# Six layers of local attention: the value and output weights of a head as one matrix

## The chip, the cores and the metric

The kernel runs on one core of a Trainium2 chip. The metric is the device time of one execution in microseconds (us); the kernel before has a median of 3638.47 us over 3 runs (3638.31 to 3640.38). Engine names are those of the profile: PE (matmul) and PEld (its weight loads), DVE (vector), ACT (scalar), POOL (GpSimd) and SP, which issues the transfers (DMA).

## The reference

The input is 8 sequences of 512 tokens with 128 features, all in float32. A first attention with polynomial weights and a normalisation comes first; the change leaves its computation alone. Then six layers follow, each of a local attention and a gated feed-forward part. The attention of a layer is what changes:

```python
DIM = 128; DEPTH = 6; HEADS = 16; DIM_HEAD = 64; WINDOW = 32; INNER = HEADS * DIM_HEAD

def local_attention(q, k, v):          # windows of 32 queries, each sees its own and the
    ...                                # previous window: 64 keys
    sim = jnp.einsum('bhwie,bhwje->bhwij', bq, bk2) * QK_SCALE
    sim = jnp.where(mask, -jnp.finfo(sim.dtype).max, sim)
    attn = jax.nn.softmax(sim, -1)
    out = jnp.einsum('bhwij,bhwje->bhwie', attn, bv2)
    return out.reshape(b, h, n, d)

def attn_layer(x, Wqkv, qs, ksc, Wo):
    qkv = x @ Wqkv
    q, k, v = jnp.split(qkv, 3, -1)
    ...
    q = l2norm(q) * qs
    k = l2norm(k) * ksc
    ...                                # rotary turn of q and k
    out = local_attention(q, k, v)
    out = out.transpose(0, 2, 1, 3).reshape(b, n, INNER)
    return out @ Wo
```

In the loop over layers, attention and feed-forward part each add their result to x after half of the features of x have been shifted by one token (the kernel keeps x shifted in `state`).

For one head the output is softmax(S) (X Wv) Wo, and by the rules of matrix products this equals (softmax(S) X) (Wv Wo). Wv of a head is 128 x 64 and Wo 64 x 128, so Wv Wo is 128 x 128.

## The kernel before

`state[b]` holds a sequence with its 128 features on partitions and 512 tokens along the row. The work of the six layers is cut into 192 units: 6 layers, 8 sequences, 4 blocks of 128 tokens (`j`). A loop over slots `t` (L766) runs a software pipeline: in slot `t` each step works on the unit `t - lag`, as written `at(t, lag, step)`. The order of PE's instructions is exactly that of the program (`manual_schedule`, L757); the other engines are ordered by the framework's scheduler, with a few orders forced by `issue_behind` (L87). A slot holds, in PE's order:

- `proj` (lag 0, L439): q and k of a unit, two matmuls of 512 columns each, into PSUM tiles of the tag "mm". DVE multiplies them by two rotary tables (L459, L467), ACT squares them (L475), POOL adds the two products (L482). Later DVE sums the squares (`sum_squares`), ACT and POOL form the lengths and POOL scales (`unit_length`, L498).
- `by_keys` (lag 2, L594): 8 transposes of the softmax weights `pe`, in two PSUM tiles of the tag "tr", each copied by ACT to `pT`.
- `out_project` (lag 3, L637): 8 matmuls with `wo` into `py`, a PSUM tile of the tag "s"; DVE adds the two halves to `state` (L647).
- `by_features` (lag 1, L532): 16 transposes of q and k, in four "tr" tiles, each copied by ACT (L548). Between them lie `weigh_values` (lag 2, L604), 64 small matmuls of 64 rows and 32 columns, into `po` of the tag "s", which DVE divides by the softmax sums (L621), and `values` (lag 0, L502), the projection of v into an "mm" tile.
- `spread` (lag 0, L512): ACT copies v; eight DMAs (seven where a block is the first of its sequence) lay out the 64 keys of each window in `v2`.
- for the last block of a sequence, one part of the feed-forward step in each of four slots: `feed_norm`, `feed_first`, `feed_middle` (12 matmul instructions of 512 columns), `feed_last`.
- `scores` (lag 1, L563): 64 small matmuls that add to a mask which ACT has put into `sp` (`masked`, L553, tag "s"). DVE takes the maxima (L580), ACT makes 16 exps with the maxima as bias (L584), DVE sums (L590) and inverts (L591).
- `out_by_features` (lag 2, L627): 8 transposes of the divided result `on`, copied by ACT to `oT` (L635).

PSUM is handed out by tags: "mm" has two buffers of two banks, "tr" two buffers of one bank, "s" one of two banks. A new tile of a tag takes the buffer of the one before last ("mm", "tr") or the last ("s"), and its first matmul waits until that one's readers are done. Every float32 matmul of the program is two matmul instructions on PE, each with its weight load; a transpose is one.

Two calls of `addr_align` in the slot loop (L780, L782) and two in `feed_hidden` move the address of PE's next instruction to a multiple.

Of the kernel before, what the change touches and what calls it, by code (L numbers as in the profile page):

```python
# [28 lines left out]
def sandwich_kernel(ctx: ExitStack, tc: tile.TileContext, ins: dict, out: bass.AP):  # L29
# [5 lines left out]
    DEPTH = ins["L0_ffn_Wqkv"].shape[0]  # L35
# [16 lines left out]
    x1 = [dram.tile([P, NB, DM], F32, tag=f"x1_{b}", name=f"x1_{b}") for b in range(B)]  # L52
    roots = [dram.tile([2, 2, 2, N], F32, tag=f"roots_{i}", name=f"roots_{i}") for i in range(2)]
    state = [const.tile([P, N + 1], F32, tag=f"state_{b}", name=f"state_{b}") for b in range(B)]
    for b in range(B):
        nc.vector.memset(state[b][HD:P, 0:1], 0.0)

# [95 lines left out]
    tw = wl.tile([P, 3, 2, 512], F32, tag="wqkv", name="tw")  # L153
# [4 lines left out]
    nc.sync.dma_start(tw[:, 2], a_w[:, 2])  # L158
# [3 lines left out]
    woT = tw[:, 2].rearrange("p s (c d) -> p (s c) d", d=DM)  # L162
# [200 lines left out]
    def to_state(b):  # L363
        xs = bt[b].pop("xs")
        ps = psum.tile([P, NB, P], F32, tag="tr", name="tr")
        for j in range(NB):
            transposed(ps[:, j, :], xs[:, j, :], P, P)
        pf = ps.rearrange("p a b -> p (a b)")
        for a in range(2):
            r = slice(HD * a, HD * (a + 1))  # L370
            nc.vector.tensor_copy(state[b][r, a : N + a], pf[r])

# [36 lines left out]
    def load_layer(l):  # L409
        wqkv = wl.tile([P, 3, 2, 512], F32, tag="wqkv", name=f"wqkv_{l}")  # L410
        nc.sync.dma_start(
            wqkv, ins["L0_ffn_Wqkv"][l].rearrange("p (t s c) -> p t s c", t=3, s=2)
        )
        wo = wl.tile([P, NP, DM], F32, tag="wo", name=f"wo_{l}")
        nc.sync.dma_start(wo, ins["L0_ffn_Wo"][l].rearrange("(c p) d -> p c d", p=P))
# [21 lines left out]
        return dict(wqkv=wqkv, wo=wo, w1=w1, w2=w2, tab=tab)  # L437

    def proj(u, s):  # L439

        L, b, j = u["L"], u["b"], u["j"]
        wqkv, tab = L["wqkv"], L["tab"]
# [7 lines left out]
        for a in range(2):  # L450
            nc.tensor.matmul(  # L451
                ps[:, a].rearrange("p h d -> p (h d)"), lhs, wqkv[:, s, a, :], start=True, stop=True
            )
# [30 lines left out]
    def sum_squares(u, s):  # L484
        su = nc.vector.tensor_reduce(  # L485
            u["ss"][:, s], u["sq", s].rearrange("p h a d -> p h (a d)"), AX.X, ALU.add
        )
        if divisions:
            issue_behind(su, divisions[-1])
# [12 lines left out]
    def values(u):  # L502
        L, b, j = u["L"], u["b"], u["j"]
        lhs = state[b][:, j * P : (j + 1) * P]

        v0 = f3.tile([P, 2, 512], F32, tag="v0", name="v0")
        ps = psum.tile([P, 2, 512], F32, tag="mm", name="mm")
        for p in range(2):
            nc.tensor.matmul(ps[:, p, :], lhs, L["wqkv"][:, 2, p, :], start=True, stop=True)  # L509
        u["v0"], u["v0ps"] = v0, ps  # L510

    def spread(u):  # L512
        j, v0 = u["j"], u["v0"]
        cp = nc.scalar.copy(v0, u.pop("v0ps"))
        if copies:
            issue_behind(cp, copies[-1])

        v2 = f2.tile([P, 4, 512], F32, tag="v2", name="v2")
        for p in range(2):
            if j == 0:  # L520
                nc.gpsimd.memset(v2[HD * p : HD * p + W, 0, :], 0.0)
            else:
                nc.sync.dma_start(v2[HD * p : HD * p + W, 0, :], u["B"]["v0"][P - W : P, p, :])
            nc.sync.dma_start(v2[HD * p + W : HD * (p + 1), 0, :], v0[0:W, p, :])
            for w in range(1, 4):
                nc.sync.dma_start(
                    v2[HD * p : HD * (p + 1), w, :], v0[W * (w - 1) : W * (w + 1), p, :]
                )
        u["B"]["v0"] = v0
        u["v2"] = v2  # L530
# [32 lines left out]
    def scores(u):  # L563
# [18 lines left out]
        for pair in range(NP):  # L582
            for p in range(2):
                ex = nc.scalar.activation(  # L584
                    pe[:, pair, p, :], sp[:, p, pair, :], AF.Exp, bias=mx[:, p, pair : pair + 1]
                )
                issue_behind(ex, tables[-1])
# [4 lines left out]
        u["pe"], u["su"] = pe, su  # L592
# [11 lines left out]
    def weigh_values(u):  # L604


        v2, pT, su = u["v2"], u["pT"], u["su"]
        po = psum.tile([P, 2, NP, HD], F32, tag="s", name="po", bufs=1)
        for pair in range(NP):
            for w in range(4):  # L610
                for p in range(2):
                    r = slice(HD * p, HD * (p + 1))
                    nc.tensor.matmul(  # L613
                        po[W * w : W * (w + 1), p, pair, :],
                        pT[r, pair, W * w : W * (w + 1)],
                        v2[r, w, HD * pair : HD * (pair + 1)],
                        start=(pair == 0), stop=True, skip_group_check=True,
                    )
        u["on"] = on = f1.tile([P, NP, 2, HD], F32, tag="on", name="on")
        with tc.high_priority():  # L620
            dv = nc.vector.tensor_tensor(  # L621
                on.rearrange("t c p d -> t p c d"), po,
                su.rearrange("t c p -> t p c").unsqueeze(3).to_broadcast([P, 2, NP, HD]), ALU.mult,
            )
        divisions.append(dv)

    def out_by_features(u):  # L627
        on = u["on"]
        u["oT"] = oT = f1.tile([P, NP, P], F32, tag="oT", name="oT")
        for c in range(0, NP, 4):  # L630
            ps = psum.tile([P, 4, P], F32, tag="tr", name="tr")
            for i in range(4):
                transposed(ps[:, i, :], on[:, c + i].rearrange("p a d -> p (a d)"), P, P)
            with tc.high_priority():
                nc.scalar.copy(oT[:, c : c + 4, :], ps)  # L635

    def out_project(u):  # L637

        L, b, j, oT = u["L"], u["b"], u["j"], u["oT"]
        py = psum.tile([P, P], F32, tag="s", name="py", bufs=1)  # L640
        for c in range(NP):
            nc.tensor.matmul(py, L["wo"][:, c, :], oT[:, c, :], start=(c == 0), stop=(c == NP - 1))  # L642
# [114 lines left out]
    with tc.manual_schedule(engines={mybir.EngineType.PE}):  # L757
# [8 lines left out]
        for t in range(len(units) + 7):  # L766
            if t < len(units):
                u = units[t]
                if u["l"] not in layers:
                    layers[u["l"]] = load_layer(u["l"])  # L770
                u["L"] = layers[u["l"]]


            gelus = 0 <= t - 5 < len(units) and units[t - 5]["j"] == NB - 1
            at(t, 0, proj, 0)
            at(t, 0, proj, 1)


            if t % NB == 1 and NB < t < len(units):
                nc.tensor.addr_align(128, offset=IN_STEP)  # L780
            if t % NB == 3 and NB < t < len(units):
                nc.tensor.addr_align(FILL)  # L782
            at(t, 2, by_keys)
            if gelus:
                gelu_only()
            at(t, 3, out_project)
# [3 lines left out]
            if t == 1:  # L790
                attn_out(B - 1)
            at(t, 1, by_features, 0)
            at(t, 2, weigh_values)
# [135 lines left out]
```

## Time and profile before

| | |
|---|---|
| median of 3 runs | 3638.47 us (3638.31 to 3640.38) |
| profiled execution, span | 3641.2 us |
| first attention | 0 to about 479 us |
| six layers, begin (479 to 583 us) | PE busy 84.99 of 104.00 us |
| six layers, steady (583 to 3560 us) | PE busy 2969.12 of 2977.00 us; DVE 2416.28, ACT 2419.42, POOL 1754.86 |
| last 81.2 us | PE busy 59.49 us |
| clock granted to PE, mean | 0.993 |
| transfers | 250.73 MB, mean 69 GB/s |

The rows of a profile give the start and the length of a group of equal instructions, the engine, the line of the program, what is written and read with its shape (partitions x elements; for PE the rows and columns of the array), and the count. In brackets stands the time for which the engine stood idle before the group, and what released it. The rows of the layers' costliest groups on the other engines:

```profile
L482 POOL TENSOR_TENSOR qk<-t,t 128x1024 f32<-128x1024 f32 x384 | 910.9, 2372 | 619.1 <-DVE t L467 424.7
L498 POOL TENSOR_TENSOR qk<-qk,ss 128x1024 f32<-128x1024 f32 x384 | 722.4, 1902 | 16.0
L584 ACT ACTIVATE pe<-sp,mx 128x64 f32<-128x64 f32 x3072 | 652.0, 381 | 2.4 <-DVE mx L580 2.3
L635 ACT COPY oT<-tr 128x512 f32<-128x512 f32 x384 | 205.5, 587 | 168.1 <-PE tr L70 165.5
```

Each gives the busy time in all, the mean of one in ns, and the idle time before. Other rows used later: L514 (v copy, 128x1024) 1019 ns; L558 (mask, 128x1024) 1028; L548 (copies of q and k, 128x512) 589; L475 (squares, 128x512) 605; L316 (square of 128x1024) 1057; L621 (division, 128x1024) 1225; L459 and L467 1219; L647 (64x128) 284.

### The profile page before, as it was taken

What the parts mean: (1) busy time and instruction counts of PE and PEld (TensorE: products, weight loads), DVE (VectorE), ACT (ScalarE), POOL (GpSimd) and SP (SyncE); (2) the same over time, 40 slices, a digit from 0 to 9 for tenths busy, and PEclk for the clock granted to TensorE, in tenths of its full rate; (3) what the DMA queues carried; (4) which work ended last, traced back from release to release, by engine and by line L of the source; (5) the groups of instructions that cost most, each with busy time, mean ns of one, the idle gap of its engine ahead of it and who ended that gap; (6) DMA issues with size and microseconds to landing.
All of it is one profiled execution on the core that took longest, in us unless ns stands there. A gap on an engine that the chain in (4) does not pass through costs nothing.

```text
span 3641.2 us, 153034 instructions
## 1 busy us (share of the span) xinstructions
PE 3575.2 (98%) x65184; PEld 2404.3 (66%) x65184; DVE 2796.4 (77%) x3915; ACT 2765.6 (76%) x6864; POOL 1843.6 (51%) x1311
## 2 busy tenths in 40 slices
PE   8999989999999999999999999999999999999997
PEld 4555556666766666676766766667676676766765
DVE  4555567887878788787887878878787887878885
ACT  4555557787888888888787888888878787887875
POOL 0000045555655556555565655556555565556652
PEclk9999999999999999999999999999999999999998
DMA  3121132222232222232222322223222222222221
GB/s 109 46 53 47 42 89 68 65 65 69 79 77 72 65 64 71 77 81 68 61 69 68 87 72 69 65 65 86 71 71 69 60 70 64 66 68 73 74 74 47
DMA packets 158598, 250.73 MB, mean 69 GB/s; under 512 B 33774, under 2 KB 54508, under 8 KB 157164
## 3 DMA queue, kind: packets, MB, share of 16 engines
q1 hardware_dynamic: 157932, 240.93, 25.2%
q8 instruction: 530, 8.68, 1.0%
q14 instruction: 136, 1.11, 0.1%
HBM read 41.31 MB, written 4.46 MB: 13 GB/s over the span
## 4 chain that ended last, share of the span: by engine, by line
PE 87%; ACT 9%; DVE 2%; issue 1%; DMA 1%; POOL 0%; SPq 0%; POOLq 0%; DVEq 0%; ACTq 0%
PE tr L70 19%; PE mm L451 14%; PE py L642 10%; PE mm L509 9%; PE po L613 8%; PE sp L572 6%; ACT pe L584 4%; PE mm L667 4%; PE mm L669 4%; PE y L299 3%; PE py L702 3%; PE sc L269 2%; PE po L348 2%; ACT L76 1%; PE vv L247 1%; ACT oT L635 1%
## 5 line engine op out<-in xcount | busy, mean ns | idle before, releaser
L482 POOL TENSOR_TENSOR qk<-t,t 128x1024 f32<-128x1024 f32 x384 | 910.9, 2372 | 619.1 <-DVE t L467 424.7
L498 POOL TENSOR_TENSOR qk<-qk,ss 128x1024 f32<-128x1024 f32 x384 | 722.4, 1902 | 16.0
L451 PE MATMUL mm<-wqkv,state 128*128 128x512 f32 x1536 | 700.3, 596 | 0.6 <-issue 0.6
L584 ACT ACTIVATE pe<-sp,mx 128x64 f32<-128x64 f32 x3072 | 652.0, 381 | 2.4 <-DVE mx L580 2.3
L459 DVE TENSOR_TENSOR t<-mm,tab 128x1024 f32<-128x1024 f32 x384 | 468.3, 1219 | 220.3 <-PE mm L451 214.9
L475 ACT ACTIVATE sq<-mm 128x512 f32<-128x512 f32 x768 | 420.6, 605 | 127.4 <-DVE t L467 120.9
L467 DVE TENSOR_TENSOR t<-mm,tab 128x1024 f32<-128x1024 f32 x384 | 468.1, 1219 | 5.9
L451 PEld LDWEIGHTS mm<-wqkv,state 128*128 128x128 f32 x1536 | 273.1, 190 | 289.8 <-issue 242.4
L485 DVE TENSOR_REDUCE ss<-sq 128x16 f32<-128x1024 f32 x384 | 448.4, 1209 | 0.1
L70 PE MATMUL tr<-ident,qk 128*128 128x128 f32 x3072 | 440.9, 276 | 1.8 <-ACT qT L548 0.8
L70 PEld LDWEIGHTS tr<-ident,qk 128*128 128x128 f32 x3072 | 351.3, 141 | 120.7 <-issue 56.3
L642 PE MATMUL py<-oT,wo 128*128 128x128 f32 x3072 | 379.3, 277 | 0.3 <-ACT oT L635 0.3
L642 PEld LDWEIGHTS py<-oT,wo 128*128 128x128 f32 x3072 | 368.1, 196 | 0.5 <-ACT oT L635 0.5
L509 PE MATMUL mm<-wqkv,state 128*128 128x512 f32 x768 | 362.9, 595 | 2.6 <-DVE t L467 2.6
L635 ACT COPY oT<-tr 128x512 f32<-128x512 f32 x384 | 205.5, 587 | 168.1 <-PE tr L70 165.5
L572 PEld LDWEIGHTS sp<-kT,qT 64*32 64x32 f32 x24576 | 264.2, 105 | 91.3 <-issue 54.3
L613 PE MATMUL po<-v,pT 64*32 64x64 f32 x24576 | 297.0, 225 | 9.6 <-issue 3.9
L548 ACT COPY qT<-tr 128x512 f32<-128x512 f32 x384 | 226.3, 589 | 99.6 <-PE tr L70 99.1
L613 PEld LDWEIGHTS po<-v,pT 64*32 64x32 f32 x24576 | 268.8, 105 | 46.0 <-PE tr L70 24.6
L572 PE MATMUL sp<-kT,qT 64*32 64x64 f32 x24576 | 297.6, 225 | 0.3 <-issue 0.3
L495 POOL TENSOR_SCALAR ss<-ss 128x32 f32<-128x32 f32 x192 | 54.7, 285 | 478.7 <-ACT ss L98 470.8
L548 ACT COPY kT<-tr 128x512 f32<-128x512 f32 x384 | 225.6, 588 | 74.8 <-PE tr L70 74.5
(110 smaller groups left out, 5243.9 us busy)
## 6 DMA issues: line engine op xcount, KB each, us to landing
v<-v SPq DMA_DIRECT2D x1152, 128.0 KB
v<-v SPq DMA_DIRECT2D x672, 64.0 KB
rs<-roots SPq DMA_DIRECT2D x64, 256.0 KB
wqkv<-in_L_ffn_Wqkv_dram SPq DMA_DIRECT2D x6, 1536.0 KB
wo<-in_L_ffn_Wo_dram SPq DMA_DIRECT2D x6, 512.0 KB
xin<-_attn_hidden_states_dram SPq DMA_DIRECT2D x8, 256.0 KB
xr<-_attn_hidden_states_dram SPq DMA_DIRECT2D x8, 256.0 KB
x<-xr SPq DMA_DIRECT2D x8, 256.0 KB
```

Source lines behind the costliest of these rows:

```text
L70: nc.tensor.transpose(ps[:cols, :rows], src, ident[:rows, :rows])
L451: nc.tensor.matmul(ps[:, a].rearrange("p h d -> p (h d)"), lhs, wqkv[:, s, a, :], start=True, stop=True)
L459: nc.vector.tensor_tensor(t2, ps[:, ::-1], tab[:, 2 * s + 1, j, :].rearrange("p (a d) -> p a d", a=2).unsqueeze(2) .to_broadcast([P, 2, H, ...
L467: nc.vector.tensor_tensor(t1, ps, tab[:, 2 * s, j, :].rearrange("p (a d) -> p a d", a=2).unsqueeze(2) .to_broadcast([P, 2, H, HF]), ALU.mult,)
L482: nc.gpsimd.tensor_tensor(qk[:, s].rearrange("p h a d -> p a h d"), t1, t2, ALU.add)
L498: nc.gpsimd.tensor_tensor(t, t, ss[:, i, :].unsqueeze(2).to_broadcast([P, H, HD]), ALU.mult)
L509: nc.tensor.matmul(ps[:, p, :], lhs, L["wqkv"][:, 2, p, :], start=True, stop=True)
L548: copies.append(nc.scalar.copy(dst, ps))
L572: nc.tensor.matmul(sp[W * w : W * (w + 1), p, pair, :], qT[HD * p : HD * (p + 1), pair, W * w : W * (w + 1)], kT[HD * p : HD * (p + 1), pa ...
L584: ex = nc.scalar.activation(pe[:, pair, p, :], sp[:, p, pair, :], AF.Exp, bias=mx[:, p, pair : pair + 1])
L613: nc.tensor.matmul(po[W * w : W * (w + 1), p, pair, :], pT[r, pair, W * w : W * (w + 1)], v2[r, w, HD * pair : HD * (pair + 1)], start=(pa ...
L642: nc.tensor.matmul(py, L["wo"][:, c, :], oT[:, c, :], start=(c == 0), stop=(c == NP - 1))
```

## The change

The value projection and its layout are dropped. Each layer multiplies the value and output weights of every head once (`value_weights` loads them, `value_products` makes 16 matrices of 128 x 128, `wm`). The softmax weights are divided by their sums before they are transposed (POOL), and then weigh the tokens themselves: `windows` reads, for every window, its 64 tokens from a copy of the sequence in DRAM (`xtok`), `weigh_tokens` multiplies, and `out_project` sends the 16 results through the 16 matrices. `to_tokens` writes the copy in DRAM after each layer. The 16 exps become a subtraction on DVE and one exp. `py` moves from the tag "s" to the tag "tr". The softmax steps get one slot more of lag, the two `addr_align` of the slot loop go, and the weights of a layer are loaded in the middle of the layer before.

```diff
+    xtok = [dram.tile([W + N + 1, DM], F32, tag=f"xtok_{b}", name=f"xtok_{b}") for b in range(B)]
...
     def load_layer(l):
-        wqkv = wl.tile([P, 3, 2, 512], F32, tag="wqkv", name=f"wqkv_{l}")
...
-        wo = wl.tile([P, NP, DM], F32, tag="wo", name=f"wo_{l}")
...
+        wqk = wl.tile([P, 2, 2, 512], F32, tag="wqk", name=f"wqk_{l}")
...
+    def value_weights(l):
+
+        wv = f1.tile([P, NP, DM], F32, tag="on", name="wv")
+        wo = f1.tile([P, NP, DM], F32, tag="oT", name="wo")
+        for s, t in enumerate((wv, wo)):
+            nc.sync.dma_start(t.rearrange("p c d -> p (c d)"), ins["L0_ffn_Wvo"][l, s])
+        wm = wl.tile([P, 2, NP, DM], F32, tag="wm", name=f"wm_{l}")
...
+    def value_products(l):
+        L = layers[l]
+        for c in range(0, NP, 4):
+            ps = psum.tile([P, 2, 4, DM], F32, tag="mm", name="wm")
+            for i in range(4):
+                for p in range(2):
+                    r = slice(HD * p, HD * (p + 1))
+                    nc.tensor.matmul(
+                        ps[:, p, i, :], L["wv"][r, c + i, :], L["wo"][r, c + i, :], start=True, stop=True,
+                        skip_group_check=True,
+                    )
+            nc.scalar.copy(L["wm"][:, :, c : c + 4, :], ps)
...
     def sum_squares(u, s):
...
-        if divisions:
-            issue_behind(su, divisions[-1])
...
-    def values(u):
...
-    def spread(u):
-        j, v0 = u["j"], u["v0"]
-        cp = nc.scalar.copy(v0, u.pop("v0ps"))
-        if copies:
-            issue_behind(cp, copies[-1])
...
+    def windows(u):
+
+        b, j = u["b"], u["j"]
+        t = f3.tile([P, 2, 512], F32, tag="v0", name="xw")
+        u["xw"] = xw = t[:, 0].rearrange("p (w d) -> p w d", d=DM)
+        x0 = xtok[b][j * P : j * P + W + P, :]
         for p in range(2):
...
+            nc.sync.dma_start(
+                xw[HD * p : HD * (p + 1)],
+                bass.AP(tensor=x0.tensor, offset=x0.offset, ap=[[DM, HD], [W * DM, 4], [1, DM]]),
+            )
+
+    def to_tokens(u):
+
+        b = u["b"]
+        ps = psum.tile([P, NB, P], F32, tag="tr", name="tr")
+        for j in range(NB):
+            transposed(ps[:, j, :], state[b][:, j * P : (j + 1) * P], P, P)
+        xt = f2.tile([P, N], F32, tag="ge", name="xt")
+        nc.scalar.copy(xt, ps.rearrange("p a b -> p (a b)"))
+        nc.sync.dma_start(
+            xtok[b][W : W + N, :].rearrange("(n p) d -> p n d", p=P), xt.rearrange("p (n d) -> p n d", d=DM)
+        )
...
-        for pair in range(NP):
-            for p in range(2):
-                ex = nc.scalar.activation(
-                    pe[:, pair, p, :], sp[:, p, pair, :], AF.Exp, bias=mx[:, p, pair : pair + 1]
-                )
-                issue_behind(ex, tables[-1])
+        with tc.high_priority():
+            nc.vector.tensor_tensor(
+                pe.rearrange("t c p k -> t p c k"), sp,
+                mx.unsqueeze(3).to_broadcast([P, 2, NP, 2 * W]), ALU.add,
+            )
+        pf = pe.rearrange("t c p k -> t (c p k)")
+        ex = nc.scalar.activation(pf, pf, AF.Exp)
+        issue_behind(ex, tables[-1])
...
+        divisions.append(
+            nc.gpsimd.tensor_tensor(pe, pe, su.unsqueeze(3).to_broadcast([P, NP, 2, 2 * W]), ALU.mult)
+        )
...
-    def weigh_values(u):
...
-    def out_by_features(u):
...
+    def weigh_tokens(u, half):
+
+        xw, pT = u["xw"], u["pT"]
+        if half == 0:
+            u["zT"] = f2.tile([P, 2, NP, P], F32, tag="v2", name="zT")
+        zT = u["zT"]
+        ps = psum.tile([P, 2, NP, 2 * W], F32, tag="mm", name="z")
+        for i in range(2):
+            w = 2 * half + i
+            for p in range(2):
+                r = slice(HD * p, HD * (p + 1))
+                nc.tensor.matmul(
+                    ps[:, p, :, W * i : W * (i + 1)], xw[r, w, :], pT[r, :, W * w : W * (w + 1)],
+                    start=(i == 0), stop=True, skip_group_check=True,
+                )
+        nc.scalar.copy(
+            zT[:, :, :, HD * half : HD * (half + 1)].rearrange("f p c t -> f (p c) t"),
+            ps.rearrange("f p c t -> f (p c) t"),
+        )
 
     def out_project(u):
 
-        L, b, j, oT = u["L"], u["b"], u["j"], u["oT"]
-        py = psum.tile([P, P], F32, tag="s", name="py", bufs=1)
-        for c in range(NP):
-            nc.tensor.matmul(py, L["wo"][:, c, :], oT[:, c, :], start=(c == 0), stop=(c == NP - 1))
+        L, b, j, zT = u["L"], u["b"], u["j"], u["zT"]
+        py = psum.tile([P, P], F32, tag="tr", name="py")
+        for p in range(2):
+            for c in range(NP):
+                nc.tensor.matmul(
+                    py, L["wm"][:, p, c, :], zT[:, p, c, :],
+                    start=(p + c == 0), stop=(p + c == NP),
+                )
...
-        for t in range(len(units) + 7):
+        for t in range(len(units) + 8):
...
+                if t % (NB * B) == NB * B // 2 and u["l"] + 1 < DEPTH:
+                    layers[u["l"] + 1] = load_layer(u["l"] + 1)
+                    value_weights(u["l"] + 1)
...
-            if t % NB == 1 and NB < t < len(units):
-                nc.tensor.addr_align(128, offset=IN_STEP)
-            if t % NB == 3 and NB < t < len(units):
-                nc.tensor.addr_align(FILL)
-            at(t, 2, by_keys)
+            at(t, 3, by_keys)
...
-            at(t, 3, out_project)
+            at(t, 4, out_project)
...
             at(t, 1, by_features, 0)
-            at(t, 2, weigh_values)
+            at(t, 3, weigh_tokens, 0)
             at(t, 1, by_features, 4, 0)
             at(t, 1, masked)
-            at(t, 0, values)
+            at(t, 3, weigh_tokens, 1)
...
             at(t, 1, by_features, 4, 1)
-            at(t, 0, spread)
...
+            at(t, 2, windows)
...
+            if t % (NB * B) == NB * B - 3 and t < len(units) and u["l"] + 1 < DEPTH:
+                value_products(u["l"] + 1)
...
+            if t < 8 + NB * B * (DEPTH - 1):
+                at(t, 8, to_tokens, ends=True)
             at(t, 1, scores)
...
-            at(t, 2, out_by_features)
```

The other steps of the feed-forward part and of the output follow with one slot more of lag. `to_state` also writes the first copy of the tokens to DRAM; the first layer's products are made in slot 2.

## The prediction

> **What bounds the kernel now.** I read the page's busy times and chain first, then TensorE's timeline of the layer stage, then two places where it stands still. In the page the reader is to see that PE is taken 98% of the span and that the chain stays on PE for 87% of it; of ACT's 9% the next view shows why it is not idle PE.
>
> ```profile
> PE 3575.2 (98%) x65184; PEld 2404.3 (66%) x65184; DVE 2796.4 (77%) x3915; ACT 2765.6 (76%) x6864; POOL 1843.6 (51%) x1311
> PE 87%; ACT 9%; DVE 2%; issue 1%; DMA 1%; POOL 0%; SPq 0%; POOLq 0%; DVEq 0%; ACTq 0%
> ```
>
> TensorE's timeline of one slot (one unit of each lag; the six feed-forward matmul groups are left out). Matmul spans overlap at their ends, so a group's cost is its start to the next group's start.
>
> ```profile
> 2028.17 3.60 PE L451 MATMUL mm<-wqkv,state 128*128 128x512 f32 x8
> 2031.61 1.06 PE L70 MATMUL tr<-ident,pe 128*128 128x128 f32 x8
> 2032.51 1.95 PE L642 MATMUL py<-oT,wo 128*128 128x128 f32 x16
> 2034.30 1.04 PE L70 MATMUL tr<-ident,qk 128*128 128x128 f32 x8
> 2035.38 1.58 PE L613 MATMUL po<-v,pT 64*32 64x64 f32 x128
> 2036.89 0.66 PE L70 MATMUL tr<-ident,qk 128*128 128x128 f32 x4
> 2037.38 1.88 PE L509 MATMUL mm<-wqkv,state 128*128 128x512 f32 x4
> 2039.10 0.60 PE L70 MATMUL tr<-ident,qk 128*128 128x128 f32 x4
> ...
> 2045.08 1.58 PE L572 MATMUL sp<-kT,qT 64*32 64x64 f32 x128
> 2046.59 1.09 PE L70 MATMUL tr<-ident,on 128*128 128x128 f32 x8
> 2047.52 3.60 PE L451 MATMUL mm<-wqkv,state 128*128 128x512 f32 x8
> ```
>
> Differences of starts: 3.44 + .90 + 1.79 + 1.08 + 1.51 + .49 + 1.72 + .44 + 1.51 + .93 = 13.81 us a slot, without a gap. Other engines are hidden; only PE's sum and new gaps in it count. There are 192 units (6 layers, 8 batches, 4 blocks).
>
> **PE work.** Removed per unit: the value projection (L509, 1.72), the weighing of values (L613, 1.51) and the transposes of `on` (.93): 4.16. Added: out_project goes from 8 to 16 products, one more 1.79. weigh_tokens has 8 products with 64 rows, 128 columns and 256 moving columns, each two instructions as every f32 product here. A pass of 512 columns costs .43 (3.44/8), of 256 so .215. The trace has no 64x128 tiles; the nearest rows are the attention stage's row tiles (32x128) and column tiles (128x64):
>
> ```profile
> 411.45 1.51 PE L299 MATMUL y<-am,tv 128*64 128x384 f32 x8
> 412.90 0.93 PE L269 MATMUL sc<-tq,tk 32*128 32x384 f32 x8
> 413.75 1.98 PE L238 MATMUL qk<-xlT,tw 128*128 128x512 f32 x4
> ```
>
> Eight passes of 384 columns would be 2.58 one by one. They took .85 in four row tiles (two sets at .32 plus .21) and 1.45 in two column tiles (four at .32 plus .17). So tiles run side by side and a burst costs about .2 more: a half of weigh_tokens is 4 x .215 + .2 = 1.05 and both 2.1. Ends: .86 a half if the extra vanishes, 1.9 if the two tiles take turns. I take 1.05, because both neighbours overlap fully. Work alone: -4.16 + 1.79 + 2.1, and .11 less where `po` no longer stands between transposes: about -.38 a unit, -73 us over 192.
>
> [...]
>
> **New gaps in PE.** Moving `py` from its own buffer ("s") into the two "tr" buffers is what I price highest. The order in a slot becomes: transposes of the first four pairs of pe (buffer 1), of the second four (buffer 2), py (buffer 1 again), four transposes of q (2), four of k (1, now held by py). Before, py lay elsewhere, and 1.79 of py or 1.5 of po always stood between the two uses of a buffer. How long a buffer needs after its last matmul shows where PE had nothing else to do:
>
> ```profile
> 506.13 0.60 PE L70 MATMUL tr<-ident,qk 128*128 128x128 f32 x4
> 507.49 0.63 PE L70 MATMUL tr<-ident,qk 128*128 128x128 f32 x4 [0.77 <-ACT qT L548]
> 508.80 0.66 PE L70 MATMUL tr<-ident,qk 128*128 128x128 f32 x4 [0.68 <-ACT kT L548]
> ```
> ```profile
> 3613.03 0.49 PE L70 MATMUL nx<-ident,state 128*128 128x128 f32 x3
> 3613.24 0.59 DVE L647 TENSOR_TENSOR state<-py,state 64x128 f32<-64x128 f32 x2 [1.70 <-PE py L642]
> 3613.88 0.33 PE L70 MATMUL nx<-ident,state 128*128 128x128 f32 x1 [0.36 <-DVE state L647]
> ```
>
> Four transposes plus ACT's copy (589 ns) turn a buffer round in 1.31; .44 is PE's own, so it is free .87 after its last transpose. py now comes .44 after it: a gap of .43. In the second view py ends at about 3612.93 (the weight loads of the next group start there), DVE adds both halves, and PE goes on at 3613.88: .95. Only the four q transposes (.44) cover it: a gap of .51. Together .94 a unit, 180 us. Ends: the first 0 to 1.0 (ACT may be in a 605 ns square), the second .2 to 1.7 (DVE may be in a 1219 ns product). I take the bare turn-rounds, since ACT and DVE have idle time in the slot. Queued behind DVE's wait for py are proj's products of the second half and the sums of squares, and behind those POOL's L482; PE asks for that PSUM buffer again at the second half of weigh_tokens, 3 us later.
>
> **ACT, DVE, POOL.** ACT loses 16 exps (16 x 381 overlapped, 3.39 by the timeline, 652 us in all), the v copy (1019) and two oT copies (587 each); it gains one exp of 128x1024 (nearest row: Square of that shape, 1057) and two z copies (1019 each): about -2.5 a unit. DVE swaps the division (1225) for the subtraction of the maximum (same shape, 1225). POOL gains one 128x1024 product (L498's 1902; L482's 2372 as the other end) on a 51% engine, and loses small memsets. None of these times is on PE's path by itself: 11 to 13 us a slot each against 14. Their latency (maximum, subtraction, exp, sum, reciprocal, POOL product: 1.2 + 1.2 + 1.1 + 1.2 + .25 + 1.9 = 6.9) is covered by by_keys moving one slot later; without that slot it would exceed proj's 3.44 by 3.5 a unit. It removes PE's present wait for the exps in the slots after gelus (at 2050.96 eight transposes take 1.17 rather than .90): 48 x .27 = -12 us.
>
> But ACT's work bunches at the slot's end. Between z0 and the scores' second half it copies z0 (1.02), q (.59), fills the mask (1.03) and copies k (.58), with z1's copy (1.02) free to come before k's; the line that put the v copy behind k's copy is gone. Where a slot has the long feed-forward matmuls before the scores this is covered; in one of four only .5 us of transposes lie there, and in the gelu slot a PSUM buffer waits for z1's copy. I take 1.0 for four slots, 48 us; ends 0 and 154 (.8 in every slot).
>
> **Transfers and small steps.** Per unit eight SBUF copies of v (some 1 MB) become two reads of DRAM (256 KB), one slot before use; SP, which now waits 911 us on PE for L523, becomes lighter. Cover: a whole slot of 14 us. If a transfer took longer, PE would wait for xw. The write of tokens to DRAM lies 23 slots before its first reader. Weight loads move to the middle of the layer before: nothing, as PE waits for no weights now either. to_tokens: 40 x .44 = 18 us. value_products: 16 products of 64x128 by 128 a layer, 2.2 (16 pairs at .112 and two bursts' .2), 6 x 2.2 = 13; one by one 22. One slot more of fill and drain: 10 (0 to 20; the drain's chain is longer by the POOL product and the longer py).
>
> **Instruction supply.** The slots' two alignments go. How PE starves without them shows in the first slots, which never had any:
>
> ```profile
> 521.47 1.22 PE L613 MATMUL po<-v,pT 64*32 64x64 f32 x102
> 524.59 0.43 PE L613 MATMUL po<-v,pT 64*32 64x64 f32 x26 [1.90 <-issue]
> ```
>
> Between 513 and 583 us such gaps and one stretched L509 add to .64 + 1.90 + 1.45 + .31 + 1.97 = 6.3 in five slots, 1.25 a slot. The fetches are 530 of 8.68 MB, 16 KB or 256 instructions of 64 bytes. From the burst's start to its resumption pass 3.1 us, so I reckon a block used up faster than that runs dry. Only blocks that begin within some 46 of the new slot's 416 instructions are that quick (the scores' 256 alone in 1.5 us): 46/256 of a start a slot, .8 short on average, .14 a slot, 27 us. Ends: 0 and the old rate, 240. [...]
>
> **Sum.** -73 + 180 - 12 + 48 + 18 + 13 + 10 + 27 = +211. On the profiled span of 3641.2 that is 3852; the median of the runs, 3638.47, lies 2.7 lower: **3850 us**.
>
> **Rivals.** *A, no gaps, faster:* ACT and DVE release the "tr" buffers within the .44 that covers them. Then gaps and bunching (228) go, and with no starving (27) the sum is -44: 3595. It decides only if both releases come under .44; the 1.31 turn-round and the .95 speak against it. Chance .07. *B, row tiles of 64 take turns:* weigh_tokens costs 1.9 a half, +1.7 a unit, +326: 4175. Speaks for it: no such tile in the trace; against: both neighbours. Chance .08. *C, starving at the old rate:* +213: 4060. For: no alignment is left in the slot; against: one dense burst rather than two. Chance .07. *D, only one of the two gaps or neither bunching:* about 3640 to 3720, the PE saving nearly paid back. Chance .08, of it .03 within .2% of before. The forecast, gaps in every slot: .70, with its own range 3720 to 4020.
>
> The chances: faster by over .2% (7 us, about what these runs can tell from no change) .08, within it .03, slower .89. The range 3720 to 4020 leaves .2 outside.
>
> **What would show it.** Right: gaps of about .4 ahead of py released by ACT's pT copy, and of .5 ahead of k's transposes released by DVE's state; py groups of 3.58; z groups near 1.05; ACT well under 76%; PE's busy share below 95%. Wrong: PE without gaps (A), z groups near 1.9 (B), long `issue` gaps inside the scores (C). A scheduling of ACT or DVE that answers py a whole operation late would put the time above 4000.

## The result and the profile after

The kernel after takes **4052.3 us** (median of 4 runs, 4047.59 to 4053.91), the kernel before beside it 3638.73 us (4 runs, 3638.31 to 3640.38). The ratio is 1.1132, 95% interval 1.1117 to 1.1148: slower by 413.6 us where 211 were forecast. The profiled execution has a span of 4052.1 us at a mean granted clock of 0.987 (before: 3641.2 at 0.993).

The page of the kernel after, busy times and the chain that ended last:

```profile
PE 3712.4 (92%) x44800; PEld 2488.4 (61%) x44800; DVE 2785.3 (69%) x3916; ACT 2356.4 (58%) x3844; POOL 2140.6 (53%) x1407
PE 70%; ACT 15%; DVE 9%; issue 4%; DMA 1%; POOL 1%; SPq 0%; POOLq 0%; DVEq 0%; ACTq 0%
```

PE lost a third of its instructions and 6 points of its busy share, and the chain now leaves PE for ACT and DVE in a quarter of the span. PE's idle time went from 66.0 us (3641.2 - 3575.2) to 339.7 (4052.1 - 3712.4). That is 274 of the 411 us between the two spans; the other 137 stand as more busy time, although the work per unit fell. Part of it is the new steps `to_tokens` and `value_products`, and part is how the rows are made: a group's span reaches some .1 to .2 us into what follows it (in the view below .16 at `proj`, 3.70 long and 3.54 from start to start), so that a gap shows as idle time only past that tail. A gap is read from start to start, not from the bracket.

PE's timeline of one slot of the kernel after (start, length, line, operation, count; in brackets the idle time and its releaser), the one in which `feed_norm` (`nx`) and `to_tokens` run, then the scores and the next slot's `proj`:

```profile
2207.72 3.70 PE L479 MATMUL mm<-wqk,state 128*128 128x512 f32 x8
2211.26 1.04 PE L75 MATMUL tr<-ident,pe 128*128 128x128 f32 x8
2212.53 3.84 PE L655 MATMUL py<-zT,wm 128*128 128x128 f32 x32 [0.24 <-ACT pT L627]
2216.21 0.60 PE L75 MATMUL tr<-ident,qk 128*128 128x128 f32 x4
2217.15 0.63 PE L75 MATMUL tr<-ident,qk 128*128 128x128 f32 x4 [0.34 <-DVE state L663]
2217.70 1.13 PE L640 MATMUL z<-pT,xw 64*128 64x256 f32 x8
2218.77 0.66 PE L75 MATMUL tr<-ident,qk 128*128 128x128 f32 x4
...
2220.91 0.60 PE L75 MATMUL nx<-ident,state 128*128 128x128 f32 x4
2221.35 0.60 PE L75 MATMUL tr<-ident,state 128*128 128x128 f32 x4
2222.06 0.86 PE L592 MATMUL sp<-kT,qT 64*32 64x64 f32 x64
2223.49 0.86 PE L592 MATMUL sp<-kT,qT 64*32 64x64 f32 x64 [0.57 <-ACT kT L568]
2224.28 1.98 PE L479 MATMUL mm<-wqk,state 128*128 128x512 f32 x4
2228.14 1.98 PE L479 MATMUL mm<-wqk,state 128*128 128x512 f32 x4 [1.88 <-DVE xn L117]
```

Four things are to be seen. The two forecast gaps are there: 1.27 from `tr<-pe` to `py` instead of .90, and .94 from the q transposes to the k transposes instead of .44. A half of `weigh_tokens` costs 1.07. The scores wait between their halves for ACT's copy of k. And the second half of the next slot's `proj` comes 3.86 us after the first instead of some 1.7: it waits for `xn`, a product of the feed-forward norm on DVE, which the forecast didn't mention. DVE's timeline in that stretch shows why `xn` is late:

```profile
2224.46 1.23 DVE L600 TENSOR_REDUCE mx<-sp 128x16 f32<-128x1024 f32 x1 [1.74 <-PE sp L592]
2225.60 0.40 DVE L117 TENSOR_SCALAR xn<-nx,ln_mv,ln_rs 128x128 f32<-128x128 f32 x1
2225.92 1.22 DVE L603 TENSOR_TENSOR pe<-sp,mx 128x1024 f32<-128x1024 f32 x1
2227.05 1.04 DVE L117 TENSOR_SCALAR xn<-nx,ln_mv,ln_rs 128x128 f32<-128x128 f32 x3
```

After the maxima DVE makes one of the four `xn`, then the new subtraction (1.22), then the other three. `nx` and `proj`'s second half share the two "mm" buffers, so PE waits until the last `xn` has read `nx`, at 2228.09. ACT's bunching is in its timeline of the same slot:

```profile
2220.98 1.03 ACT L578 CAST sp<-mask 128x1024 f32<-128x1024 bf16 x1
2221.93 1.02 ACT L644 COPY zT<-z 128x1024 f32<-128x1024 f32 x1
2222.83 0.61 ACT L568 COPY kT<-tr 128x512 f32<-128x512 f32 x1
```

The second copy of `zT`, which only the next slot's `out_project` needs, stands ahead of `kT`, which PE needs at once. PE's waits over the whole span (total us, how often, longest):

```profile
PE mm L479 <- DVE xn L117: 86.9, 46, 2.2
PE sp L592 <- ACT kT L568: 51.6, 98, 0.6
PE tr L75 <- DVE state L663: 48.4, 143, 0.3
PE py L655 <- ACT pT L627: 48.3, 178, 1.6
PE tr L75 <- ACT qT L568: 36.7, 48, 0.8
```

These five are 272 us, nearly all of the 274 of added idle time. Mean lengths of the four kinds of slot between 1000 and 3300 us, worked out from starts of `proj`, show where each falls; a sequence has one of each, 48 in all:

| slot, by its part of the feed-forward | before | after | change |
|---|---|---|---|
| `feed_last` | 16.68 | 17.35 | +.67 |
| `feed_norm` (and `to_tokens`) | 14.13 | 16.56 | +2.43 |
| `feed_first` (opens with the late `xn`) | 14.24 | 18.78 | +4.54 |
| `feed_middle` | 19.31 | 19.94 | +.63 |
| sum | 64.36 | 72.63 | +8.27 |

48 x 8.27 is 397 us, and six times `value_products` (2.7 each) 16: the whole 413. So the loss is in the steady slots, and more than half of it in the slot that waits for `xn`.

### The profile page after: what moved, and what is told of

It is laid out like the page before. It is cut to its first block, busy times and chain, and to the rows that moved or that the text cites. A ratio compares the mean times of both kernels' runs of the same rounds, so it can differ in the third digit from the quotient of the medians.

```text
span 4052.1 us, 105065 instructions
## 1 busy us (share of the span) xinstructions
PE 3712.4 (92%) x44800; PEld 2488.4 (61%) x44800; DVE 2785.3 (69%) x3916; ACT 2356.4 (58%) x3844; POOL 2140.6 (53%) x1407
## 4 chain that ended last, share of the span: by engine, by line
PE 70%; ACT 15%; DVE 9%; issue 4%; DMA 1%; POOL 1%; SPq 0%; POOLq 0%; DVEq 0%; ACTq 0%
PE py L655 18%; PE mm L479 15%; PE tr L75 8%; PE z L640 6%; PE sp L592 5%; ACT zT L644 5%; PE y L305 3%; PE mm L683 3%; PE py L718 3%; PE mm L685 3%; DVE ss L513 3%; ACT pT L627 3%; ACT sp L578 2%; PE sc L275 2%; DVE state L663 2%
## 5 line engine op out<-in xcount | busy, mean ns | idle before, releaser
L479 PE MATMUL mm<-wqk,state 128*128 128x512 f32 x1536 | 737.4, 618 | 90.4 <-DVE xn L117 86.9
L655 PE MATMUL py<-zT,wm 128*128 128x128 f32 x6144 | 738.4, 278 | 48.5 <-ACT pT L627 48.3
L655 PEld LDWEIGHTS py<-zT,wm 128*128 128x128 f32 x6144 | 702.0, 192 | 94.4 <-ACT pT L627 93.9
L479 PEld LDWEIGHTS mm<-wqk,state 128*128 128x128 f32 x1536 | 272.6, 190 | 405.8 <-issue 250.2
L640 PE MATMUL z<-pT,xw 64*128 64x256 f32 x3072 | 436.2, 403 | 2.3 <-ACT sq L503 2.1
L644 ACT COPY zT<-z 128x1024 f32<-128x1024 f32 x384 | 389.6, 1015 | 25.4 <-PE z L640 23.4
L615 POOL TENSOR_TENSOR pe<-pe,su 128x1024 f32<-128x1024 f32 x192 | 365.7, 1904 | 13.0 <-PE z L640 10.5
L600 DVE TENSOR_REDUCE mx<-sp 128x16 f32<-128x1024 f32 x192 | 235.2, 1225 | 170.0 <-PE sp L592 166.5
L640 PEld LDWEIGHTS z<-pT,xw 64*128 64x128 f32 x3072 | 265.1, 186 | 84.3 <-issue 47.0
L627 ACT COPY pT<-tr 128x512 f32<-128x512 f32 x384 | 207.3, 588 | 180.8 <-PE tr L75 180.7
```

What stands on the lines that cost most here:

```text
L479: nc.tensor.matmul(ps[:, a].rearrange("p h d -> p (h d)"), lhs, wqk[:, s, a, :], start=True, stop=True)
L640: nc.tensor.matmul(ps[:, p, :, W * i : W * (i + 1)], xw[r, w, :], pT[r, :, W * w : W * (w + 1)], start=(i == 0), stop=True, skip_group_che ...
L644: nc.scalar.copy(zT[:, :, :, HD * half : HD * (half + 1)].rearrange("f p c t -> f (p c) t"), ps.rearrange("f p c t -> f (p c) t"),)
L655: nc.tensor.matmul(py, L["wm"][:, p, c, :], zT[:, p, c, :], start=(p + c == 0), stop=(p + c == NP),)
```

## The experiments

The theory after the two traces were compared: four causes, each of which can be taken out by itself. **Two gaps around `py`** (its place in the "tr" buffers), **ACT's order** (copy of `zT` ahead of `kT`), **DVE's order** (subtraction ahead of `xn`). The rival: these waits only hide one another, so that a gap taken out shows up at the next one and little is gained. Times below are medians of 4 runs; the ratio is to the kernel before, run beside it on the same chip (3641.99 us for e1 to e4, 3643.21 for e5 to e8, 3642.64 for e9).

**e1: `py` in a buffer of the tag "s" again.** It shares the one buffer of this tag with the scores. Judged by the values that come out, a part of the scores seems to be left without its mask in this kernel and in e4; PE's instructions are as many as in the kernel after (44800).

```diff
     def out_project(u):
-        py = psum.tile([P, P], F32, tag="tr", name="py")
+        py = psum.tile([P, P], F32, tag="s", name="py", bufs=1)
```

> The changed kernel with py back in its own buffer (tag s). Theory of the two gaps: the .37 us ahead of py (ACT's pT copy) and the .50 ahead of the transposes of k (DVE's state) go in all 190 slots, 165 us: 4052 becomes 3887 (3870 to 3910). Rival, the gaps only hide work of DVE and ACT that is late anyway: PE then waits for the same engines a little later in the slot, and less than 80 us go: 3970 or more.

Measured: 3887.98 us, 1.0675 (1.0659 to 1.0691): 164 less than the kernel after. Its PE timeline:

```profile
2216.46 1.04 PE L75 MATMUL tr<-ident,pe 128*128 128x128 f32 x8
2217.34 3.74 PE L655 MATMUL py<-zT,wm 128*128 128x128 f32 x32
2220.91 1.04 PE L75 MATMUL tr<-ident,qk 128*128 128x128 f32 x8
```

From `tr<-pe` to `py` pass .88, and the eight transposes of q and k run in one piece. Both gaps are gone; the wait for `xn` ahead of these rows is 1.88 us as before the edit. 164 us is the price of `py`'s place.

**e2: ACT copies k ahead of the second half of z.**

```diff
     def weigh_tokens(u, half):
...
-        nc.scalar.copy(
+        u["z", half] = ps
+        if half == 0:
+            copy_tokens(u, 0)
+    def copy_tokens(u, half):
+        cp = nc.scalar.copy(
...
+        if half:
+            issue_behind(cp, copies[-1])
...
             at(t, 1, by_features, 4, 1)
+            at(t, 3, copy_tokens, 1)
```

> The changed kernel with ACT's copy of the second half of z put behind its copy of k. Theory of the bunching: the waits inside the scores for ACT's k copy (.57 and .48 us, with the later start .8 and .7, in two slots of four) go, 48 x 1.5 = 72 us: 3980 (3970 to 4000). Rival, z's copy is needed at once: PE waits for the mm buffer of z in the gelu slots or at proj instead, and the time stays within 20 us of 4052.

Measured: 3987.57 us, 1.0947 (1.0929 to 1.0965): 65 less than after. The wait for `kT` is no longer among PE's waits; what is left at that place is

```profile
PE sp L592 <- issue: 14.4, 9, 2.4
PE sp L592 <- ACT ss L103: 11.5, 43, 1.1
```

and the wait for `xn` has hardly changed (79.2 us after 86.9). The first of these rows, 14.4 us in 9 places, is `issue`: PE waited for nothing that the profile shows. Here and below such rows are read as PE starving for its own instructions, an estimate from the places at which they fall (last section). The kernel after has no such row there.

**e3: DVE makes all four `xn` ahead of the subtraction.**

```diff
     def scores(u, t):
...
             maxima.append(nc.vector.tensor_reduce(mx, sp, AX.X, ALU.max, negate=True))
+        with tc.high_priority():
+            at(t, 4, feed_normed, ends=True)
         with tc.high_priority():
-            nc.vector.tensor_tensor(
+            sb = nc.vector.tensor_tensor(
                 pe.rearrange("t c p k -> t p c k"), sp,
...
+        if normed[0] is not None:
+            issue_behind(sb, normed[0])
```

> The changed kernel with DVE's subtraction of the maximum put behind the four normalising products of the feed-forward step (xn). Theory: the wait in the middle of proj in the slot after feed_norm (2.35 us more than in the other slots, 47 times) holds the 1.22 us of the subtraction, which stands between the first and the other three xn: 47 x 1.22 = 57 us go, 3995 (3980 to 4005). Rival, the wait is for the maxima, which came late since the scores ended late: nothing goes, 4052 within 10; or the subtraction's delay moves the wait to the transposes of pe, with the same outcome.

Measured: 3978.95 us, 1.0924 (1.0907 to 1.094): 73 less than after, 16 more than expected. Its timeline, DVE and PE together:

```profile
2188.44 1.23 DVE L603 TENSOR_REDUCE mx<-sp 128x16 f32<-128x1024 f32 x1 [1.74 <-PE sp L595]
2189.59 1.36 DVE L119 TENSOR_SCALAR xn<-nx,ln_mv,ln_rs 128x128 f32<-128x128 f32 x4
2191.00 1.98 PE L482 MATMUL mm<-wqk,state 128*128 128x512 f32 x4 [0.75 <-DVE xn L119]
```

The four `xn` run in one piece right behind the maxima, and PE's wait falls from 1.88 to .75. It does not vanish: `xn` still stands behind the maxima, as it did in the kernel before:

```profile
2013.00 1.09 PE L70 MATMUL tr<-ident,on 128*128 128x128 f32 x8
2013.18 1.23 DVE L580 TENSOR_REDUCE mx<-sp 128x16 f32<-128x1024 f32 x1
2013.93 3.79 PE L451 MATMUL mm<-wqkv,state 128*128 128x512 f32 x8
2014.32 1.36 DVE L112 TENSOR_SCALAR xn<-nx,ln_mv,ln_rs 128x128 f32<-128x128 f32 x4
```

There the transposes of `on` stand ahead, and PE's eight matmuls run without a gap: 3.63 us for this `proj` (3.44 in the other slots), against 4.57 here and 5.89 in the kernel after.

Waiting for `xn` fell by 52 us (86.9 to 34.9); most of what is left of the 73 can be PE's clock. In the kernel after, from 583 us to the last 70, the granted clock is .5 in 13 stretches of 3.4 us, and each begins .7 to 1.4 us after PE has waited 1.88 us for `xn`. By an estimate at most 22 us go with them (13 x 3.4 x .5). e3, whose longest wait for `xn` is 1.1 us, has no such stretch there, nor has the kernel before.

**e4: all three.** The edits of e1, e2 and e3 together.

> The changed kernel with all three edits. Theory of separate waits: they add, 4052 - 165 - 72 - 57 = 3758 (3735 to 3790), still slower than before, since PE's own work per slot is not less than before. Rival of one late chain (DVE and ACT, each wait hides the next): clearly less than the sum goes, 3820 or more. Rival that the waits alone make the loss: the time comes below 3640.

Measured: 3766.72 us, 1.0342 (1.0327 to 1.0357): 286 less than after, where the three alone sum to 164 + 65 + 73 = 302. They add up within 16 us; the rival, that the waits hide one another, falls. The 16 may be the clock: of the 13 stretches at half clock e2 has 3 left and e3 none, a gain of 17 to 22 us in each that e4 can make only once. But the kernel is still 125 us slower than before. Of the wait for `xn` 29.3 us are left.

**e5: other work between the uses of the buffers.** `py` stays in "tr", as the change has it; PE's order is changed, with e2's and e3's edits.

```diff
             at(t, 0, proj, 0)
-            at(t, 0, proj, 1)
             at(t, 3, by_keys)
+            at(t, 0, proj, 1)
...
             at(t, 4, out_project)
...
-            at(t, 1, by_features, 0)
             at(t, 3, weigh_tokens, 0)
-            at(t, 1, by_features, 4, 0)
+            at(t, 1, by_features, 0)
             at(t, 1, masked)
             at(t, 3, weigh_tokens, 1)
+            at(t, 1, by_features, 4, 0)
```

> The changed kernel with py left in the two tr buffers, but with other work of PE between their uses: the second half of proj between the transposes of pe and py, and the first half of z between py and the transposes of k; also with the orders of the two runs before (k's copy first, xn first). Theory that a tr buffer needs about .87 to .95 us after its last matmul and that only cover was missing: the gaps ahead of py and of k's transposes vanish (below .1 us a slot) and the time is that of the run with py in its own buffer and the same two orders, 3767 (3740 to 3800). Rival, py in tr makes PE wait wherever it stands (DVE and ACT answer late): the gaps move to other steps and the time stays above 3850.

Measured: 3793.86 us, 1.0416 (1.0399 to 1.0432). Its PE timeline:

```profile
2217.97 1.04 PE L75 MATMUL tr<-ident,pe 128*128 128x128 f32 x8
2218.84 1.88 PE L482 MATMUL mm<-wqk,state 128*128 128x512 f32 x4
2220.56 3.73 PE L670 MATMUL py<-zT,wm 128*128 128x128 f32 x32
2224.22 1.13 PE L648 MATMUL z<-pT,xw 64*128 64x256 f32 x8
2225.29 1.09 PE L75 MATMUL tr<-ident,qk 128*128 128x128 f32 x8
```

The time is inside the range, 27 us above the 3767 expected and as much above e4. Half of `proj` covers the turn-round ahead of `py`, half of `weigh_tokens` the one behind it, and no gap stands at either. So the gaps come from the order of the uses of a buffer, not from `py` being in "tr" as such. What is new is a wait of the transposes for ACT's copy of q:

```profile
PE tr L75 <- ACT qT L571: 88.9, 96, 1.2
```

**e6: the kernel before with the subtraction and one exp.** This is the part of the change that DVE's order is about, alone, in the kernel before.

```diff
-        for pair in range(NP):
-            for p in range(2):
-                ex = nc.scalar.activation(
-                    pe[:, pair, p, :], sp[:, p, pair, :], AF.Exp, bias=mx[:, p, pair : pair + 1]
-                )
-                issue_behind(ex, tables[-1])
+        with tc.high_priority():
+            nc.vector.tensor_tensor(
+                pe.rearrange("t c p k -> t p c k"), sp,
+                mx.unsqueeze(3).to_broadcast([P, 2, NP, 2 * W]), ALU.add,
+            )
+        pf = pe.rearrange("t c p k -> t (c p k)")
+        ex = nc.scalar.activation(pf, pf, AF.Exp)
+        issue_behind(ex, tables[-1])
```

> The kernel before with one part of the change alone: the subtraction of the maximum on DVE and one exp in place of 16. Theory that the subtraction, standing among the xn products, is what holds proj's PSUM buffer in the slot after feed_norm: 48 x 1.2 = 57 us more there, less the .27 x 48 = 13 us for which PE now waits for the exps: 3638 + 44 = 3682 (3660 to 3700). Rival, the wait in the changed kernel comes from the missing .93 us of transposes between scores and proj alone: no more wait here, 3625 (3615 to 3640).

Measured: 3853.33 us, 1.0583 (1.055 to 1.0615): +210, where 44 were expected. Its timeline has the wait for `xn`:

```profile
2116.27 1.88 PE L451 MATMUL mm<-wqkv,state 128*128 128x512 f32 x4
2116.66 0.40 DVE L112 TENSOR_SCALAR xn<-nx,ln_mv,ln_rs 128x128 f32<-128x128 f32 x1
2116.98 1.22 DVE L583 TENSOR_TENSOR pe<-sp,mx 128x1024 f32<-128x1024 f32 x1
2118.11 1.04 DVE L112 TENSOR_SCALAR xn<-nx,ln_mv,ln_rs 128x128 f32<-128x128 f32 x3
2119.21 1.98 PE L451 MATMUL mm<-wqkv,state 128*128 128x512 f32 x4 [1.05 <-DVE xn L112]
```

So the wait comes with the subtraction and the one exp alone, without `py`, tokens or a longer lag. The rest of the 210 is something that no theory named; PE's waits:

```profile
PE po L615 <- issue: 105.4, 57, 4.0
PE mm L451 <- DVE xn L112: 49.5, 47, 1.1
```

PE starves for instructions (`issue`) inside the small matmuls of `weigh_values`, 105.4 us against 3.9 in the kernel before, though no matmul was added or taken away (65184 in both). A third row has PE wait 24.1 us at `po` for its own transposes (.8 before), and the granted clock is .984 instead of .993, by an estimate 36 us (.016 x 3848 less .007 x 3641). Together these come to about the 210.

**e7: the same, with `xn` ahead of the subtraction** (e6 with e3's edit).

> As the run before, with the subtraction put behind the four xn products. Theory: the 57 us go again and the 13 us of exp waits stay saved: 3625 (3610 to 3640), the fastest of all. Rival: the later subtraction makes exp, and so the transposes of pe, late in that slot (it would end 6 us after the scores, with proj's 3.44 and the .93 as cover): 3640 to 3680.

Measured: 3796.33 us, 1.0425 (1.0398 to 1.0451). The total missed for the same reason as e6: 77.8 us of starving at `po`. The difference between e6 and e7 is the expected 57 us, but 28 of it are less starving (105.4 - 77.8), so that its size proves little. What counts is that PE's 49.5 us of waiting for `xn` are gone from its waits at `proj` altogether, as the order on DVE says. The rival's wait is there too, but small: the transposes of `pe` wait for the later exp 17.6 us in 50 places (6.6 in 3 in e6).

**e8: the kernel before without the slots' two alignments.**

```diff
-            if t % NB == 1 and NB < t < len(units):
-                nc.tensor.addr_align(128, offset=IN_STEP)
-            if t % NB == 3 and NB < t < len(units):
-                nc.tensor.addr_align(FILL)
```

> The kernel before without the two address alignments of the slot loop. Theory of the prediction: PE then starves as in the first slots, where two dense bursts a slot stand, about 1.25 us a slot: 190 x 1.25 = 240 us, 3880 (3750 to 3900). Rival, most block crossings are hidden and the first slots starved for another reason (the weight transfers): 3640 to 3670.

Measured: 3750.12 us, 1.0293 (1.0274 to 1.0311): +107, .56 a slot, between the expectations. PE's waits:

```profile
PE po L613 <- issue: 53.1, 25, 2.6
PE tr L70 <- issue: 20.1, 15, 2.3
```

The alignments are worth 107 us in the kernel before: PE's `issue` rows come to 93 us (9 in the kernel before), and the granted clock is .987 instead of .993, by an estimate 23 us. In the kernel after, which has none in its slot loop, PE has .9 us of `issue` at `proj` and in no other place.

**e9: e5 with `feed_first` and `to_tokens` behind the scores.** To give `xn` and ACT's copies more room.

```diff
-            at(t, 5, feed_first, ends=True)
...
-            if t < 8 + NB * B * (DEPTH - 1):
-                at(t, 8, to_tokens, ends=True)
-            at(t, 1, scores, t)
+            at(t, 1, scores, t)
+            at(t, 5, feed_first, ends=True)
+            if t < 8 + NB * B * (DEPTH - 1):
+                at(t, 8, to_tokens, ends=True)
```

> As the reordered kernel (3794), with feed_first and to_tokens put behind the scores, so that the tr buffer they take has had 1.4 us since its copy was asked for; before the scores PE waits there for ACT's q copy, .65 us in one slot of four and 1.23 in another, and in the same slot .3 for z. Theory that what is left above the kernel before is mostly waits: 48 x 2.1 = 100 us go, 3695 (3680 to 3720), and what stays, some 50 us, is PE's own work (a slot without waits is no shorter than before, and to_tokens and the products of a layer come on top: 27 + 17 us). Rival, DVE answers feed_first late behind the maxima and the subtraction: a wait of .7 us or more at the next transposes of pe, 3740 or more. Rival that the removed work does shorten the slot: below 3640.

Measured: 3771.24 us, 1.0354 (1.0337 to 1.0371): 23 less than e5, not the expected 99. The transposes of `feed_first` and `to_tokens`, once moved, no longer stand between the transposes of k and the scores, and the scores wait for the copy:

```profile
PE sp L595 <- ACT kT L571: 58.5, 91, 0.9
```

The wait moved on to ACT. Neither the theory nor its rivals had this: the time lies where the first rival put it, but its wait, at the transposes of `pe`, is not among PE's larger waits. The run still gives a size that the account below needs: its slots with `feed_last` have no wait, and they last 16.24 us.

## Why the prediction was wrong

The direction was right and the two gaps that it priced highest were right in place, releaser and size. The size was off by 202 us. Term by term, as predicted and as the runs have it:

| term | predicted | measured | from |
|---|---|---|---|
| PE work | -73 | about -35 | e9's slot without a wait, 16.24, against 16.42 before, x 192 |
| two gaps around `py` | +180 | +164 | e1 |
| waits for exps | -12 | -14 | .87 against 1.16, 48 times |
| ACT bunching | +48 | 85 | e2: 65; q's copy in the `feed_first` slot, .42 x 48 = 20 |
| proj's wait for `xn` | 0 | 110 | 5.89 against 3.54 for `proj`, 47 times; e3: 73 |
| `to_tokens` | +18 | 28 | 40 x .71 |
| `value_products` | +13 | 18 | five of 2.69 and one of 4.4 |
| instruction supply | +27 | about 1 | .9 of issue waits at `proj` |
| fill and drain | +10 | not separated | |

The measured terms sum to 357; some 56 us of the 413 belong to no term. The rows of ACT and `xn` both hold part of the half-clock stretches of e3, so that up to 17 us may be counted twice, and the rest be as much larger. What it is stays open. One count given ahead is off, though no term rests on it: `spread` of the kernel before issues ten transfers a unit, not eight, and eight, not seven, in a sequence's first block (1152 + 672 in the trace).

**The step that failed** is the costing of DVE's new subtraction: "DVE swaps the division (1225) for the subtraction of the maximum (same shape, 1225)… None of these times is on PE's path by itself". The durations are right. But the division stood elsewhere in the slot, and the place of the subtraction is between the maxima and three of the four `xn`. DVE ran them in that order: the subtraction, 1.22 us long, starts at 2225.92 and the three `xn` behind it at 2227.05. So it costs them 1.13 us from start to start, and these hold the PSUM buffer that PE asks for at `proj`'s second half. The prediction named what is queued behind DVE's wait for `py`, and did not ask the same of the subtraction. Shown by e3 (order restored in the kernel after: -73) and by e6's timeline (subtraction and one exp alone in the kernel before: the wait appears), and by e7 (`xn` ahead of the subtraction: it is gone). e3 does not bring `proj` back to 3.54 but to 4.57. Against the 3.63 of the kernel before, the rest fits the .93 us of `out_by_features`, which stood between scores and `proj` and is gone: in e7, where it still stands there, the same order on DVE leaves no wait. e5 and e9 put .87 us of transposes back, between the halves of `proj`, with the same order on DVE: the wait for `xn`, 29.3 us in e4, is gone there, and `proj`'s second half follows the transposes after .87 to .92 us in every slot. They differ from e4 in the place of `py` and in other orders too, so this half is supported, though not by an edit that changes it alone.

**The gaps.** Forecast .43 ahead of `py` and .51 ahead of the k transposes; measured .38 and .56 (1.28 - .90; 1.50 - .94): the bare turn-rounds, .94 a unit as forecast. The price of 180 came back as 164.

**ACT bunching** was right in place and rather low in size: the 1.0 for four slots came out at 1.35 by e2 (65/48), of which up to .35 is clock (17/48), and .42 more lie in a second wait, for q's copy in the `feed_first` slot, which the prediction did not have.

**PE work** was half as good as forecast. `py`'s groups take 3.67 rather than 3.58 (3.57 in e1, where no wait stands ahead), and `proj` 3.54 rather than 3.44. `weigh_tokens` is as taken, 1.06 a half, so rival B (tiles that take turns, 1.9) falls.

**Instruction supply** costs next to nothing here (.9 us): rival C, 4060 us, gives nearly the measured time by a mechanism that the trace does not have. A total that fits is no evidence for its cause. In the kernel before, though, the alignments matter (e8: 107 us without them), so the forecast's worry was real for two dense bursts a slot.

**Rivals A and D** needed a gap or the bunching to be absent; all are there. The forecast's own test, that a time above 4000 would mean an engine answering `py` a whole operation late, was met in time and not in cause: DVE answered a whole operation late, but `xn`, not `py`.

Why did no version beat the kernel before? A slot with `feed_last` and without waits is 16.24 us against 16.42 (16.68 less its .26 of waiting for exps): the change saves PE .18 us a unit, 35 us in all, and e4 still pays 125. Sixteen products of 128 x 128 (3.67) and two halves of `weigh_tokens` (2.12) replace 1.79 + 1.51 + 1.72 + .93, about the same work.

## What to carry to other kernels

For each instruction that a change puts on an engine that runs its work in the order given, as DVE did here, list what is queued behind it there, who waits for that, and what work the same change takes from that cover: in the kernel after DVE, busy 69%, held up PE, busy 92%, for 86.9 us at `xn` alone. A "tr" buffer was free again some .87 us after the last matmul into it (ACT's copy, kernel before), and what waited for `py` could go on some .95 us after its last (DVE's two additions), so that two buffers that take turns needed as much other PE work in between; moving half a step in between (e5) closes both gaps as a buffer of its own does, though here it brought a new wait for q's copy and came out 27 us behind e4. Before the waits are mended, compare the two kernels by a slot without any: here that difference was 35 us at best.

## What the runs showed of the hardware

- Two row tiles of 64 rows by 128 columns ran side by side in the kernel after: 8 matmul instructions of 256 columns in 1.06 us, with their weight loads; by an estimate from `proj` (.215 for 256 columns) they would be 4 x .215 = .86 fully overlapped and 8 x .215 = 1.72 one by one.
- A group of 8 passes of 512 columns right behind the scores' small tiles takes 3.54 us, where 3.44 were seen behind the transposes of `on`. That what stands ahead makes the difference was not tried.
- The `issue` time depended on more than the count of instructions: 3.9 us at `po` in the kernel before, 105.4 in e6 with the same count on PE, 53.1 in e8 without alignments. It falls at a fixed distance. The kernel before has 135670 matmuls, loads and waits of PE to 530 transfers of the queue `instruction` (8.68 MB), 256 to one. Counted through its trace, four of its five `issue` gaps lie at place 193 of a 256, the fifth (3.94 us) at 165; counted in the same way, all 53 such gaps above .7 us in e8 and 45 of 51 in e6 lie at 193 or 194. In the steady part of the kernel before, the same places lie in `po` as often (185 times) and cost nothing. Why e6 starves at them stays open.
- Some waits of PE were followed by a lower clock: 13 of the 46 waits for `xn` in the kernel after (1.88 us, one 2.24) by 3.4 us at a granted clock of .5, which begins within 1.4 us; none of e3's 46, which are 1.1 us at most. The length alone does not settle it: in e2, where most of the 46 are 1.83 us, it happens once. What decides was not tried.
